# Image parts made one image further ahead, and 13 of 20 instead of 3 of 5 images in the combined form

## The chip, the cores and the metric

The kernel runs on one core of one Trainium2 chip. The metric is the device time of one execution in microseconds. The engines are named as the profile names them: PE is TensorE, PEld its weight loads, DVE is VectorE, ACT is ScalarE, POOL is GpSimd, and SP is the engine whose queue issues most of the DMAs.

## The reference

The input is 160 images of 128 channels and 32 x 32 points. Each image is normalised in groups of four channels (no scale or shift is learned), goes through a 3 x 3 convolution with padding 1, and is added to the image. Image k uses set k mod 5 of five sets of weights. The weights come from U through two steps of rounding:

```python
beta = jnp.max(U); alpha = jnp.min(U)
s1 = (beta - alpha) / 3.0
v1 = s1 * floor(U / s1)
s2 = s1 / 5.0
v2 = s2 * floor((U - v1) / s2)
w = (v1 + v2).reshape(128 * 5, 128, 3, 3)
xb = x.reshape(32, 5 * 128, 32, 32)      # gn(x) here: (g - mean) / sqrt(var + 1e-5), 32 groups
act = conv(xb, w, padding=1, feature_group_count=5)
out = x + act.reshape(160, 128, 32, 32)
```

## The kernel before

**Order of the images.** The kernel takes the images of set 0 first, then those of set 1, and so on: image i of the kernel is image i mod 32 of set i // 32. The loop in `run` has one step for each image, and all instructions are put on the engines' queues in the order in which that loop writes them; the framework adds the waits between engines from the tiles that they share. So what stands behind what on an engine is decided by the order in a step.

**Parts of an image.** The matmuls take 16-bit operands, so a normalised image is split in a high part and a low part (what the high part leaves over). An image takes one of two forms, chosen by `combined(i)`.

- *Not combined.* POOL makes the normalised image `z` (in `beside_pairs`; for the first image of a group of images ACT does it in `normalise`, with `shift` and `rstd`). ACT copies it to the high part `hi` (`high_part`). DVE makes the low part `lo` (`low_part`) and its sums and differences of neighbouring rows, `rows` (`combinations`). PE runs the high part with nine taps in each of two halves, and only the low part through the sums of rows, which need fewer products: 30 matmuls in all.
- *Combined.* The sums and differences are made first, in 32 bits, from the image itself: POOL makes part of `v` (`beside_pairs`, `outer_columns`), DVE the rest (`combine`). ACT makes the high part `vh` of all of it (`high_combined`) and DVE the low part `vl` (`low_combined`). Both parts go through the sums: 24 matmuls.

In both forms `sums_of_pairs` puts six or twelve matmuls into the banks m1a or m1b (by turns) and m2. ACT copies m2 out (`leave`), DVE makes the start of the even and odd halves of the result from both (`pairs`), PE adds the rest (`main`), and ACT copies the result out (`residual`, L926). POOL then issues a DMA that adds it to the output in memory (`accumulate`), to which SP has before stored the input itself (`store_input`).

**A step.** In step i PE makes the sums of pairs of image i+1 and `main` of image i. The parts are made ahead: `beside_pairs` and `combine` for image i+4, the high part for i+3, the low part for i+2. DVE's order in a step is: the low part of i+2, `pairs` of i+1, `combine` of i+4. ACT's order is: the sums of a later image, the result of i-1, m2 of i+1, the high part of i+3, the squares of the later image.

**Statistics.** ACT makes a sum and a sum of squares for each image (`measure`), eight early images go to DVE. `STAT_LEAD` and the expression `10 + i // 4` say how far ahead. Images come in groups (two, two, then fours up to 24, then eights) whose mean and deviation are made together in three later steps by small operations on PE, ACT, POOL and DVE. In late groups DVE ends them with `scales_by_vector` (L307, L309), which also makes `shift`.

**Weights.** The weights of a set are prepared during the set before it, in small DVE and ACT operations that `later.take` puts into the steps one by one at an even pace.

**Buffers and loads.** An image pair is one chunk of 1 MB in one of `CHUNKS` = 12 buffers. `consumed(c)` says from which step on a chunk's buffer is taken for another load. In SP's queue a load waits until the buffer's last readers are done and its store has landed; the store of a chunk waits for its load.

Of the kernel before, what the change touches and what calls it, by code (L numbers as in the profile page):

```python
# [11 lines left out]
ALU = mybir.AluOpType  # L12
# [9 lines left out]
NB = 2  # L22
# [152 lines left out]
def last_of(steps, last=None):  # L175
    for last in steps:
        pass
    return last
# [27 lines left out]
class Statistics:  # L206
# [5 lines left out]
    def __init__(self, nc, small, gavg, mhalf, nb, scale, name):  # L212
        self.nc, self.small, self.gavg, self.mhalf = nc, small, gavg, mhalf
        self.nb, self.scale, self.name = nb, scale, name
        self.late = False

        self.mv = self.tile("mv", [nb, 2])

# [85 lines left out]
    def scales_by_vector(self):  # L304

        vector = self.nc.vector
        vector.tensor_scalar_mul(self.rstd, self.rstd, self.scale)  # L307
        self.shift = self.tile("shift", [self.nb])
        vector.tensor_tensor(self.shift, self.ngm, self.rstd, ALU.mult)  # L309

    def scales(self):
        nc = self.nc
# [72 lines left out]
class Main:  # L385
# [21 lines left out]

    STAT_LEAD = 14  # L410
    LOAD_LEAD = 18
    CHUNKS = 12
    STEADY = 7
    BY_VECTOR = (8, 10, 11, 14, 19, 24, 29, 34)
    FIFTHS = 30
# [10 lines left out]
    def __init__(self, tc, ctx, keep, x, u, out):  # L426
        self.tc = tc
        nc = self.nc = tc.nc
        self.imgs, C, self.H, self.W = x.shape
        P = self.P = nc.NUM_PARTITIONS  # L430
        assert C == P and self.H * self.W == 1024
        self.per_set = self.imgs // N_SETS
        self.xv = x.rearrange("(b n) c h w -> n c b (h w)", n=N_SETS)
        self.ov = out.rearrange("(b n) c h w -> n c b (h w)", n=N_SETS)
        self.uv = u.rearrange("n (o i k) -> n o i k", o=C, k=TAPS)

        def pool(name, bufs, **kw):
            return ctx.enter_context(tc.tile_pool(name=name, bufs=bufs, **kw))

        self.const = pool("const", 1)  # L440
        self.qpool = pool("quant", 1)
        self.wpool = pool("weights", 2)
        self.upool = pool("u", 1)
        self.xpool = pool("x", self.CHUNKS)
        self.zpool = pool("z", 2)
        self.parts = pool("parts", 4)
        self.rows = pool("rows", 4)
        self.wide = pool("wide", 2)
        self.wide_parts = pool("wide_parts", 3)
        self.evac = pool("evac", 2)  # L450
        self.sums = pool("sums", 3)
        self.unread = pool("unread", 1)
        self.small = pool("small", 3)
        self.ps_eo = pool("ps_eo", 2, space=PSUM)
        ps_m = pool("ps_m", 1, space=PSUM)
        ps_small = pool("ps_small", 1, space=PSUM)
        self.steps = Steps(nc, keep)

        self.m1a, self.m1b, self.m2_ps = (
            ps_m.tile([P, self.H // 2, self.W], F32, tag=name, name=name)  # L460
            for name in ("m1a", "m1b", "m2")
        )
        self.pair = [self.m1a, self.m2_ps]

        small = ps_small.tile([P, 512], F32, tag="small", name="small")
        self.pt, self.pg = small[:, : ROW * P].rearrange("p (k o) -> p k o", k=ROW), small[:, ROW * P :]
        self.chunks, self.z, self.hi, self.v, self.eo, self.m2 = {}, {}, {}, {}, {}, {}
        self.sum, self.stored = {}, {}
        self.tables, self.wts, self.across = {}, {}, {}
        self.columns = []  # L470

        cuts = [0, 2, 4, 8, 12, 16, 20, *range(24, self.imgs + 1, 8)]
        self.groups = [range(a, b) for a, b in zip(cuts, cuts[1:])]
        self.group_of = {i: k for k, g in enumerate(self.groups) for i in g}
        self.stats = {}
# [131 lines left out]
    def stats_of(self, k):  # L607
        if k not in self.stats:
            self.stats[k] = Statistics(
                self.nc, self.small, self.gavg, self.mhalf, len(self.groups[k]),  # L610
                self.steps.lift, k,
            )
            self.stats[k].late = self.groups[k].start not in self.HURRIED
        return self.stats[k]

    def measure(self, i, stages=(0, 1)):
# [31 lines left out]
    def combined(self, i):  # L648

        if i < self.STEADY or i >= self.imgs:  # L650
            return False

        if i < self.FIFTHS:
            return i % 2 == 1
        return i % 5 % 2 == 0 if i < self.THIRDS else i % 4 != 2

    def by_scalar_too(self, i):

# [301 lines left out]
    def store_input(self, c):  # L960
# [6 lines left out]
            return  # L967
        self.stored.update((i, self.store(i)) for i in images)

    def consumed(self, c):  # L970

        return max(i + 2 if self.by_hand(i) else i - 2 for i in range(c * NB, c * NB + NB))

    def run(self):
        nc, P = self.nc, self.P
# [130 lines left out]
        for i in range(self.imgs):  # L1106
# [30 lines left out]
            else:  # L1137
                j = i - 1
                self.conv(i, on_the_way)
            ahead = i + min(10 + i // 4, self.STAT_LEAD + 1)  # L1140
            to_measure = range(measured, min(self.imgs, ahead))
            measured += len(to_measure)
            if i == 2:
# [30 lines left out]
            else:  # L1174

                last = None
                if self.combined(i + 2):
                    last = last_of(self.low_combined(i + 2))
                elif i + 2 < self.imgs:
                    self.low_part(i + 2)  # L1180
                    later.take(1)
                    last = last_of(self.combinations(i + 2))
                last = later.take(2 if self.combined(i + 2) else 1, last)
                if i + 4 < self.imgs:
                    before = self.last_but_one(last)
                    for st in scaled:
                        self.after(st.power(), before)
                    self.beside_pairs(i + 4, before)
                if i > self.FIRST and self.by_hand(j):
                    self.residual(j)  # L1190
                for k in by_scalar:
# [1 line left out]
                if i > self.FIRST and not self.by_hand(j):  # L1193
                    self.residual(j)
                    self.accumulate(j)
                part = i + 3 < self.imgs and not self.combined(i + 3)
                if i + 1 < self.imgs:
                    self.leave(i + 1)
                for st in ready:
                    if not st.late:  # L1200
                        st.deviations()
                if part:
                    if self.by_scalar_too(i + 3):
                        self.normalise(i + 3)
                    self.high_part(i + 3)
                if self.combined(i + 3):
                    self.high_combined(i + 3)
                for k in by_scalar:
                    self.measure(k, (1,))
            for st in middle:  # L1210
# [13 lines left out]
            if i >= self.FIRST:  # L1224

                if i + 1 < self.imgs:
                    self.pairs(i + 1)
                for st in scaled:
                    st.scales_by_vector()
                if self.combined(i + 4):  # L1230
                    self.combine(i + 4)
                else:
                    later.take(1)
                later.take_scalar()
                if b in (self.per_set - 4, self.per_set - 2):
                    later.finish()
                for st in ready:
                    if st.late:
                        st.deviations_by_vector()
# [65 lines left out]
```

## Time and profile before

| | us |
|---|---|
| median of 3 runs (968.45 to 969.02) | 968.95 |
| profiled execution, its own time | 968.17 |
| its span, first to last instruction | 966.4 |
| PE busy | 926.9 |
| DVE busy | 910.1 |
| ACT busy | 862.0 |
| POOL busy | 463.6 |

PE's busy time counts the time in which at least one matmul runs; matmuls overlap, and their ends are modelled. The granted clock of TensorE is 0.998 of full speed. The DMA engines are busy nine tenths or more in 32 of the 40 slices of the span, and move 263 GB/s in the mean. A load of 1 MB lands in the median 12.7 us after it is issued, a store of 1 MB 18.6 us. The time of an instruction in a row of the profile is its own duration; the next one of its engine can start up to some 0.1 us before its end.

### The profile page before, as it was taken

Reading aid. Unit: us, or ns where it says so; the run is one execution under the profiler, and the core shown is the slowest. Engines: PE = TensorE matmul, PEld = TensorE weight load, DVE = VectorE, ACT = ScalarE, POOL = GpSimd, SP = SyncE. Lnnn points to the kernel's source line nnn. Section 1 sums busy time; section 2 is a strip of 40 time slices with the busy share of each in tenths; the row PEclk is TensorE's granted clock in tenths of the full one; section 3 lists DMA queues with packets and bytes.
Section 4 is the critical chain, followed back from the end, with each engine's and each line's share of the span. In section 5 each row is a group of like instructions: output and inputs, shape, how many; then the busy total and the mean of one; then the engine's idle time right before and its main releaser. Section 6 shows DMA issues by size and latency. Waiting matters only on the chain.

```text
span 966.4 us, 13055 instructions
## 1 busy us (share of the span) xinstructions
PE 926.9 (96%) x4432; PEld 433.6 (45%) x4432; DVE 910.1 (94%) x1280; ACT 862.0 (89%) x1167; POOL 463.6 (48%) x477
## 2 busy tenths in 40 slices
PE   2999999999999999999999999999999999999997
PEld 1444444444444444444444444444444444444443
DVE  7999999999999999989999999999999998998995
ACT  5879999999999999999989999999989999998561
POOL 4345344446445444554355435534445545666550
PEclk9999999999999999999999999999999999999999
DMA  9079999999999999999999999999999999666663
GB/s 363 20 273 340 338 328 321 334 322 315 327 320 328 314 327 323 311 315 258 283 243 287 276 305 286 278 251 301 278 274 260 286 275 255 98 90 107 91 107 112
DMA packets 67450, 254.22 MB, mean 263 GB/s; under 512 B 5296, under 2 KB 5296, under 8 KB 67376
## 3 DMA queue, kind: packets, MB, share of 16 engines
q1 hardware_dynamic: 45344, 173.09, 47.6%
q0 software_dynamic: 22032, 80.23, 44.7%
q8 instruction: 36, 0.59, 0.2%
q14 instruction: 38, 0.31, 0.1%
HBM read 89.19 MB, written 164.10 MB: 262 GB/s over the span
## 4 chain that ended last, share of the span: by engine, by line


## 5 line engine op out<-in xcount | busy, mean ns | idle before, releaser
L785 PE MATMUL eo<-hi,wt 128*128 128x496 f16 (+3 forms) x1170 | 310.3, 375 | 0.9 <-ACT wt L567 0.9
L840 PEld LDWEIGHTS <-wt 128*128 128x128 f16 x1884 | 183.9, 99 | 211.5 <-DVE rows L770 1.7
L741 DVE SCALAR_TENSOR_TENSOR vl<-v,rstd,vh 128x2048 f16<-128x2048 f32 x94 | 221.5, 2356 | 1.0 <-ACT vh L735 0.9
L840 PE MATMUL eo<-vh,wt 128*128 128x512 f16 x561 | 210.2, 375 | 0.2 <-DVE eo L902 0.2
L840 PE MATMUL eo<-vl,wt 128*128 128x512 f16 x561 | 210.1, 375 | 0.0
L735 ACT ACTIVATE vh<-v,rstd 128x2048 f16<-128x2048 f32 x94 | 188.1, 2001 | 13.4 <-DVE v L694 13.0
L926 ACT COPY sum<-eo 128x1024 f32<-128x1024 f32 x153 | 160.7, 1050 | 29.4 <-PE eo L840 28.5
L675 POOL TENSOR_SCALAR v<-xt,ngm 128x64 f32<-128x64 f32 x94 | 83.0, 883 | 215.5 <-issue 66.8
L785 PEld LDWEIGHTS <-wt 128*128 128x128 f16 x1242 | 120.9, 99 | 140.2 <-DVE eo L902 2.6
L248 ACT ACTIVATE junk<-xt,mv 128x1024 uint8<-128x1024 f32 x152 | 174.4, 1147 | 0.1
L840 PEld LDWEIGHTS <-across 128*128 128x128 f16 x1128 | 110.3, 98 | 140.3 <-issue 13.3
L241 ACT ACTIVATE junk<-xt 128x1024 uint8<-128x1024 f32 x152 | 160.5, 1056 | 13.8 <-DMA xt<-in_x_dram 10.7
L711 POOL TENSOR_SCALAR z<-xt,ngm,rstd 128x1024 f32<-128x1024 f32 x49 | 90.5, 1847 | 155.9 <-DVE rows L769 45.9
L840 PE MATMUL eo<-rows,wt 128*128 128x512 f16 x378 | 143.5, 380 | 0.0
L950 POOL DMA_DIRECT2D out_dram<-sum x153 | 133.8, 876 | 9.5 <-ACT sum L926 6.1
L840 PE MATMUL m<-vl,across 128*128 128x496 f16 (+1 forms) x282 | 105.6, 374 | 9.5 <-DVE vl L741 9.5
L687 DVE TENSOR_TENSOR v<-xt 128x960 f32<-128x960 f32 x94 | 109.0, 1160 | 0.0
L840 PE MATMUL m<-vh,across 128*128 128x496 f16 (+1 forms) x282 | 105.6, 375 | 0.9 <-ACT m L888 0.9
L888 ACT ACTIVATE m<-m 128x512 f32<-128x512 f32 x157 | 93.8, 597 | 13.4 <-PE m L840 13.2
L705 POOL TENSOR_TENSOR v<-xt 128x512 f32<-128x512 f32 x94 | 97.2, 1034 | 0.0
L748 DVE TENSOR_TENSOR lo<-z,hi 128x1024 f16<-128x1024 f32 x66 | 80.6, 1220 | 0.0
L286 POOL TENSOR_TENSOR rstd<-ve,mhalf 128x8 f32<-128x8 f32 (+2 forms) x24 | 39.1, 1629 | 68.8 <-DVE rows L769 22.0
(150 smaller groups left out, 1182.3 us busy)
## 6 DMA issues: line engine op xcount, KB each, us to landing
xt<-in_x_dram SPq DMA_DIRECT2D x78, 1024.0 KB, 12.7
out_dram<-sum POOLq DMA_DIRECT2D x153, 512.0 KB, 8.8
out_dram<-xt SPq DMA_DIRECT2D x76, 1024.0 KB, 18.6
out_dram<-xt SPq DMA_DIRECT2D x7, 512.0 KB, 3.7
u<-in_L_conv_U_dram SPq DMA_DIRECT2D x4, 576.0 KB, 19.0
xt<-in_x_dram SPq DMA_DIRECT2D x4, 512.0 KB, 9.7
range<-in_L_conv_U_dram SPq DMA_DIRECT2D x3, 576.0 KB, 7.9
u<-in_L_conv_U_dram SPq DMA_DIRECT2D x2, 288.0 KB, 3.2
```

What stands on the lines that cost most here:

```text
L241: self.nc.scalar.activation(junk, image, ACTF.Copy, scale=-1.0 / image.shape[1], accum_out=self.mv[:, j, 0:1],)
L248: self.nc.scalar.activation(junk, image, ACTF.Square, bias=self.mv[:, j, 0:1], accum_out=self.mv[:, j, 1:2],)
L687: nc.vector.tensor_tensor(self.view(v, 1, (511, 2), (half, H), (1, half - 1)), self.view(x, 1, (1, 2), (W, H), (2, half - 1)), self.view(x ...
L705: ins = nc.gpsimd.tensor_sub(self.v[i][:, 1536:], odd, even)
L711: ins = nc.gpsimd.tensor_scalar(z, self.image(i), st.ngm[:, j], st.rstd[:, j], ALU.add, ALU.mult)
L735: self.nc.scalar.mul(vh, self.v[i], st.rstd[:, j])
L741: yield self.nc.vector.scalar_tensor_tensor(vl, self.v[i], st.rstd[:, j], self.hi[i], ALU.mult, ALU.subtract)
L785: nc.tensor.matmul(self.bank(target, a)[:, first:end, c0:c1], self.wts[n, col][:, k, :], tile[:, s0 : s0 + 2 * (end - first) - 1 : 2, c0 + ...
L840: self.nc.tensor.matmul(out, weights, moving, start=start and j == 0, stop=False, skip_group_check=True)
L888: self.nc.scalar.mul(m2, self.m2_ps, 0.5)
L926: nc.scalar.copy(self.as_banks(i, self.sum[i]), self.flat(i, eo))
L950: added = self.nc.gpsimd.dma_start(self.ov[n, :, b], self.sum.pop(i), accum_op=ALU.add)
```

## The change

- The parts of an image are made one image further ahead: `step_of(i, ahead)` gives the images for which a step makes a part. For early steps it is image i + ahead. In step 11 (`beside_pairs`, `combine`), 12 (high parts) and 13 (low parts) it is two images, 15 and 16. After these it is i + ahead + 1.
- `combined` takes 13 of 20 images between 30 and 130 instead of 3 of 5: 65 of 100 images instead of 60.
- `shift` is made by `scales_by_vector` only for groups whose first image is not combined; no other image reads it there. Of 19 late groups, 13 begin with a combined image.
- Images are measured one further ahead, and the lead grows faster at the start.
- The pools `rows` and `wide_parts` have one buffer more, the chunks of images one less (11), and a chunk is taken to be consumed one step earlier from image 18 on.
- Later weight steps: one after a low part and one after `combine` where two stood in a row.

```diff
-        self.late = False
+        self.late = self.shifted = False
...
-        self.shift = self.tile("shift", [self.nb])
-        vector.tensor_tensor(self.shift, self.ngm, self.rstd, ALU.mult)
+        if self.shifted:
+            self.shift = self.tile("shift", [self.nb])
+            vector.tensor_tensor(self.shift, self.ngm, self.rstd, ALU.mult)
...
-    STAT_LEAD = 14
+    STAT_LEAD = 15
+    FURTHER = 11
     LOAD_LEAD = 18
-    CHUNKS = 12
+    CHUNKS = 11
...
-        self.rows = pool("rows", 4)
+        self.rows = pool("rows", 5)
...
-        self.wide_parts = pool("wide_parts", 3)
+        self.wide_parts = pool("wide_parts", 4)
...
+            self.stats[k].shifted = not self.combined(self.groups[k].start)
...
-        return i % 5 % 2 == 0 if i < self.THIRDS else i % 4 != 2
+        return i * 13 % 20 < 13 if i < self.THIRDS else i % 4 != 2
...
+    def step_of(self, i, ahead):
+        change = self.FURTHER + 4 - ahead
+        return [k for k in range(i + ahead + (i > change), i + ahead + 1 + (i >= change)) if k < self.imgs]
...
-        return max(i + 2 if self.by_hand(i) else i - 2 for i in range(c * NB, c * NB + NB))
+        return max(i + 2 if self.by_hand(i) else i - 2 - (i > self.FURTHER + 6) for i in range(c * NB, c * NB + NB))
...
-            ahead = i + min(10 + i // 4, self.STAT_LEAD + 1)
+            ahead = i + min(10 + i // 3, self.STAT_LEAD + 1)
...
-                if self.combined(i + 2):
-                    last = last_of(self.low_combined(i + 2))
-                elif i + 2 < self.imgs:
-                    self.low_part(i + 2)
-                    later.take(1)
-                    last = last_of(self.combinations(i + 2))
-                last = later.take(2 if self.combined(i + 2) else 1, last)
-                if i + 4 < self.imgs:
+                for k in self.step_of(i, 2):
+                    if self.combined(k):
+                        last = last_of(self.low_combined(k), last)
+                    else:
+                        self.low_part(k)
+                        later.take(1)
+                        last = last_of(self.combinations(k), last)
+                last = later.take(1, last)
+                if last:
                     before = self.last_but_one(last)
                     for st in scaled:
                         self.after(st.power(), before)
-                    self.beside_pairs(i + 4, before)
+                    for k in self.step_of(i, 4):
+                        self.beside_pairs(k, before)
...
-                if part:
-                    if self.by_scalar_too(i + 3):
-                        self.normalise(i + 3)
-                    self.high_part(i + 3)
-                if self.combined(i + 3):
-                    self.high_combined(i + 3)
+                for k in self.step_of(i, 3):
+                    if self.combined(k):
+                        self.high_combined(k)
+                        continue
+                    if self.by_scalar_too(k):
+                        self.normalise(k)
+                    self.high_part(k)
...
-                if self.combined(i + 4):
-                    self.combine(i + 4)
-                else:
+                for k in self.step_of(i, 4):
+                    if self.combined(k):
+                        self.combine(k)
                     later.take(1)
```

More of the change, by code (lines that the diff above doesn't have):

```diff
@@ L1195, in run @@
                     self.accumulate(j)
-                part = i + 3 < self.imgs and not self.combined(i + 3)
                 if i + 1 < self.imgs:
```

## The prediction

> **What bounds the kernel now.** I read the page's busy line first, then the spacing of the matmuls in the timeline, then the busy time of three stretches, then the waits inside the long one. The page's first part (busy us, share of the span, instructions):
>
> ```profile
> PE 926.9 (96%) x4432; PEld 433.6 (45%) x4432; DVE 910.1 (94%) x1280; ACT 862.0 (89%) x1167; POOL 463.6 (48%) x477
> ```
>
> Three engines stand near full, so a share of the whole span decides nothing. I cut the span at the starts of `pairs` of images 3, 30, 131 and 158: the middle stretch is the one in which images 30 to 130 are made. The busy time of each engine in them:
>
> ```profile
> 56.40:222.40 166.00, 162.19 (x781) 75.85 (x780) 162.69 (x257) 153.12 (x214) 75.50 (x82) 1.00 1.04 335
> 222.40:791.80 569.40, 564.66 (x2708) 264.04 (x2707) 548.37 (x752) 545.55 (x744) 272.74 (x267) 1.00 1.02 293
> 791.80:951.70 159.90, 157.00 (x749) 73.21 (x747) 146.51 (x171) 127.38 (x153) 90.41 (x78) 1.00 0.69 126
> ```
>
> The columns are length, PE, PEld, DVE, ACT, POOL, granted clock, DMA share, GB/s. In the middle PE is idle 4.7 of 569.4 us, DVE 21.0, ACT 23.9. In the last stretch PE is idle 2.9 of 159.9 and DVE 13.4. In the first DVE is idle 3.3 of 166 and PE 3.8. So PE sets the pace from image 30 on, with DVE 3% behind it; before that DVE and PE share it. Who waits in the middle stretch (us in total, times, longest):
>
> ```profile
> DVE eo L900 <- ACT m L888: 6.0, 6, 1.4
> ...
> PE m L840 <- DVE vl L741: 4.7, 4, 1.9
> ...
> DVE twice L296 <- ACT wt L567: 3.2, 4, 1.3
> DVE eo L900 <- PE m1b L840: 2.7, 4, 1.2
> ```
>
> PE's whole idle time is one kind: the first products of an image wait for its low part `vl`, which DVE makes in the step just before. The same wait is 2.9 us (3 times) in the last stretch and 1.9 us in the first. DVE's waits are on PE, or on ACT's copy of what PE made. The small gaps between DVE's instructions are the rest: 21.0 less some 14.3 in gaps over 0.15 us leaves 6.7.
>
> **What the Trainium skill says.** "TensorE: Matmul & The Clock Gate", section "Wait — 56ns, not 53.3ns?", puts back-to-back warm matmuls at N/2.4 GHz plus about 2.5 ns, 216 ns for 512 columns. The trace agrees: twelve matmuls of a combined image start from 380.07 to 382.60, 0.211 us apart (496 and 512 columns). PE is really full, not only busy by a modelled end. "SBUF — State Buffer", section "SBUF: two separate sides", says that a DVE operation with two SBUF inputs and a GpSimd operation exclude each other for a whole instruction. The trace agrees, in the lines on `shift` below. "Perfetto Trace Analysis", section "Tensor Engine Instruction (MATMUL, LD_WEIGHTS)", says that ACT and DVE are strict first-in first-out: a late operand stops all behind it, which no run here contradicts.
>
> **The change part by part.**
>
> *Five more combined images (65 for 60 between 30 and 130).* A combined image needs 24 matmuls (two sources, `vh` and `vl`; 12 for the sums of pairs, 12 in `main`), another 30 (6, and 18 + 6). So 30 matmuls go; at the trace's 0.212 us that is **6.4 us less on PE**. DVE pays. The rows of the middle stretch:
>
> ```profile
> L741 DVE SCALAR_TENSOR_TENSOR vl<-v,rstd,vh 128x2048 f16<-128x2048 f32 x60 | 141.9, 2364 | 0.6 <-ACT vh L735 0.5
> L687 DVE TENSOR_TENSOR v<-xt 128x960 f32<-128x960 f32 x60 | 69.0, 1150 | 0.0
> L748 DVE TENSOR_TENSOR lo<-z,hi 128x1024 f16<-128x1024 f32 x40 | 48.7, 1217 | 0.0
> L694 DVE SCALAR_TENSOR_TENSOR v<-xt,twice 128x512 f32<-128x512 f32 x60 | 44.7, 744 | 0.0
> ```
>
> Combined: 2.36 + 1.15 + 0.74 = 4.26 us. Not combined: 1.22 + 0.69 (L761) + 2 x 0.42 (L769, L770) = 2.74. Five times 1.52 is **7.6 us more on DVE**. ACT: 2.00 (L735) for 1.04 (L645), five times, is +4.8; the group starts 48, 56, 88, 96 and 128 were not combined and become so, 32 and 72 and 112 the other way, so two of the 1.24 us `normalise` (L637) go: +2.3 net, inside its 23.9 idle. POOL: five times 0.90 + 1.03 for `v`, and three fewer `z` of 1.85 at most: +4 us, inside 297 of idle time.
>
> *`shift` no longer made for 13 of 19 late groups, ten of them in the middle.* Its row L309 there has 12 at a mean of 498 ns. But the timeline shows what these are:
>
> ```profile
> 443.76 1.03 POOL L705 TENSOR_TENSOR v<-xt 128x512 f32<-128x512 f32 x1
> ...
> 443.86 0.96 DVE L309 TENSOR_TENSOR shift<-ngm,rstd 128x8 f32<-128x8 f32 x1
> ...
> 444.75 1.15 DVE L687 TENSOR_TENSOR v<-xt 128x960 f32<-128x960 f32 x1
> ```
>
> `shift`, eight columns wide, ends as POOL's L705 ends; where POOL is quiet it takes 0.17 and the next starts 0.09 after it. The next, L687, has two SBUF inputs as well and would stand in the same place. So a `shift` is worth 0.09 (the block moves) to 0.50 us (it is gone), ten of them 1 to 5. I take **1 us**, since nothing in the edit moves POOL.
>
> *Parts one image further ahead from 15 or 16 on.* Step 11 does `beside_pairs` and `combine` for 15 and 16, step 12 ACT's high parts of both, step 13 the low parts of both; afterwards everything is as far apart as before, except that PE takes a part one step later (5.7 us). This takes away PE's waits for `vl`: at most 4.7 + 2.9, and in the first stretch 1.4 of the 1.9 (the other 0.5 is image 15's, whose low part stays in step 13). `rows` and `wide_parts` get one buffer more, as a part lives one step longer; that costs nothing in time. Cost: one image's low part (2.4 to 2.7 us) is pulled into a stretch where DVE has 1.2 us of gaps over 0.15, and comes back only at the end, where PE is the bound and gains nothing. If all of DVE's gaps take it, +1; if it pushes PE fully, +4 with the `combine` made early (1.9, half of the time). I take **+2**. The steeper lead of the sums and squares (`i // 3`) brings at most two images' ACT work (2 x 2.2 us) forward into ACT's 12.9 idle there: 0, at worst +4.
>
> *11 chunks for 12, each freed one image earlier.* SP's order puts load 18 behind two more 1 MB stores than before, and the image is measured one step earlier. Before, load 18 was issued at 120.3, load 19 at 135.2 and load 20 at 150.0, with 28 to 33 us to landing; moved two stores on, loads 18 and 19 stand where 19 and 20 stood, land near 163 and 178, and are wanted near 168 and 181. So a margin of 3 to 5 us where there were some 20; from load 24 on the order of the queue is the old one and 10 us remain. I take 0. If a load is late, ACT stops in its measurement with the copies and high parts of that step queued behind it, and PE waits for those: 2 to 5 us in all.
>
> *`later.take`* is spread: one weight step after the low part and one after `combine`, for two in a row. No instruction more, 0; a gain of under 1 us, from waits of a step on the one before it, is possible.
>
> **The sum**, against the profiled execution's 968.17 (966.4 span and 1.8 around it). Middle: PE's floor is 564.7 - 6.4 = 558.3. DVE's is 548.4 + 6.7 (small gaps) + 7.6 - 1 = 561.7: DVE takes over as the bound. Its waits for `wt` (3.2) have nothing to do with the change and stay: 564.9, against 569.4, is -4.5. First stretch +2. Last stretch -2.5 of its 2.9. Together -5, so 963.2; the median of 968.95 is 0.8 above the profiled execution, so **964**.
>
> **Rivals.**
> - *PE stays the bound.* The further lead lets DVE ride out its heavy steps, the `shift` savings are whole (5 us), and DVE runs with few waits: middle 558.3 to 561, last -2.9, first 0: 954 to 959. For it: all of PE's idle time had one cause, which goes. Against: DVE at 98 to 99% must meet PE twice in each step (`pairs`).
> - *DVE's waits do not shrink (the slower one).* `pairs` of an image needs PE's sums and ACT's copy m2, wherever the parts stand. If DVE's gaps over 0.15 us in the middle stay at 14.3 us, the middle takes 561.7 + 14.3 = 576.0, +6.6, and with +2 and -2.5 the kernel 975. It decides from 9 us of such gaps on: 561.7 + 9 + 2 - 2.5 is the old time. For it: 8.7 of the 14.3 are at L900, which the lead doesn't touch. Against: DVE waits there because it is early, and it will be late.
> - *Loads late* in steps 19 to 25: the forecast plus 2 to 5, 966 to 969.
> - *That it does nothing* is out: 30 matmuls are gone from PE's order.
>
> **How the numbers follow.** Forecast 0.50 (960 to 967), PE the bound 0.22, DVE's waits stay 0.18, loads late or a dearer beginning 0.10. A measurement of this kernel tells about 0.2% (1.9 us) from no change. Faster by more: all of the second, 0.46 of the first, 0.04 of the last: 0.72. Within: 0.04 of the first, 0.04 of the third, 0.05 of the last: 0.13. Slower: 0.14 of the third and 0.01 of the last: 0.15. The range 956 to 972 leaves out the best of the second and the worst of the third; the forecast's own is 960 to 967.
>
> **What would show it.** In the profile after: 30 matmuls fewer; PE's waits for `vl` gone from image 16 on; the middle some 4 to 5 us shorter with DVE's idle time down from 21 to about 10 and PE's waits for `eo` of L902 up; L687 taking some 2 us where `shift` stood; no ACT wait for `xt` after step 15. I am wrong if DVE's gaps stay above 9 us, if PE idles under 3 us in the middle, or if the first stretch grows by more than 4.

## The result, and the profile after

| us | before | after |
|---|---|---|
| median | 968.95 | 966.80 |
| lowest to highest | 968.34 to 969.48 | 965.63 to 968.85 |
| profiled execution | 968.17 | 968.85 |
| its first, middle and last stretch, and what follows the last | 166.0, 569.4, 159.9, 14.7 | 171.7, 566.8, 156.8, 15.4 |

The ratio of the times is 0.998, 95% interval 0.9972 to 0.9989: 2.15 us faster, where 5 were forecast. The profiled execution of after is the slowest of its nine. The stretches sum up (the first cut lies at 56.4 us in both): +5.7 - 2.6 - 3.1 + 0.7 = +0.7, which is 968.85 - 968.17. (The prediction calls its cuts the starts of `pairs` of images 3, 30, 131 and 158; its times are those of images 3, 30, 130 and 159, and the same images cut the stretches here.)

The page of after, busy time of each engine:

```profile
PE 922.9 (95%) x4402; PEld 430.0 (44%) x4402; DVE 913.2 (94%) x1262; ACT 863.6 (89%) x1165; POOL 469.3 (49%) x484
```

The 30 matmuls are gone (4432 to 4402). The three stretches of after (length, PE, PEld, DVE, ACT, POOL, granted clock, DMA share, GB/s):

```profile
56.40:228.10 171.70, 164.71 (x778) 75.84 (x777) 166.25 (x260) 157.89 (x220) 71.96 (x83) 0.98 1.04 338
228.10:794.90 566.80, 559.37 (x2683) 261.15 (x2682) 553.49 (x736) 547.00 (x742) 286.01 (x276) 1.00 1.02 287
794.90:951.70 156.80, 156.80 (x748) 73.13 (x747) 140.81 (x166) 122.71 (x148) 87.26 (x76) 1.00 0.71 141
```

In the middle PE works 5.3 us less than before and idles 7.4 instead of 4.7; DVE works 5.1 more and idles 13.3 instead of 21.0. In the last stretch PE never stops. The waits of the middle stretch (total, times, longest):

```profile
PEld L843 <- DVE eo L905: 12.0, 10, 2.1
...
PE eo L843 <- DVE eo L905: 7.3, 9, 1.6
DVE eo L903 <- ACT m L891: 4.4, 4, 1.3
```

No wait of PE for `vl` is left there. All of PE's idle time is now a wait for the second half of `pairs` (L905; L902 before), as the prediction said a DVE-bound middle would look. DVE's waits of 3.2 us for `wt`, which the prediction kept, are gone too.

The two rows of DVE that grew, middle stretch of after (busy, mean ns, idle before):

```profile
L744 DVE SCALAR_TENSOR_TENSOR vl<-v,rstd,vh 128x2048 f16<-128x2048 f32 x65 | 152.4, 2344 | 0.0
L690 DVE TENSOR_TENSOR v<-xt 128x960 f32<-128x960 f32 x65 | 81.6, 1256 | 0.1
```

L690's mean went from 1150 to 1256 ns, because in eight of 65 cases, at 1.92 to 2.00 us, it stands where `shift` stood. One of them in the timeline of after (start, duration):

```profile
308.61 1.03 POOL L708 TENSOR_TENSOR v<-xt 128x512 f32<-128x512 f32 x1
308.68 1.99 DVE L690 TENSOR_TENSOR v<-xt 128x960 f32<-128x960 f32 x1
```

POOL's operation ends at 309.64, and L690 needs its usual 1.15 us from about there: the block moved, as forecast.

**The beginning.** It grew by 5.7 us, not 2. That isn't an accident of this slowest execution: in e4 and e5 below, whose kernels begin alike, `pairs` of image 30 stands 5.2 and 4.9 us later than before. Two places carry it. Step 6 measures two images instead of one (`i // 3`): DVE then stands 2.36 us on ACT's copy of m2, and `pairs` of image 8 starts at 92.4 instead of 89.5. Steps 12 and 13 hold more of DVE's work than before; DVE and PE there:

```profile
125.86 1.15 DVE L690 TENSOR_TENSOR v<-xt 128x960 f32<-128x960 f32 x1
126.93 0.74 DVE L697 SCALAR_TENSOR_TENSOR v<-xt,twice 128x512 f32<-128x512 f32 x1
...
129.81 2.34 DVE L744 SCALAR_TENSOR_TENSOR vl<-v,rstd,vh 128x2048 f16<-128x2048 f32 x1
132.07 1.22 DVE L751 TENSOR_TENSOR lo<-z,hi 128x1024 f16<-128x1024 f32 x1
132.20 0.38 PE L843 MATMUL m<-vl,across 128*128 128x512 f16 x1 [2.43 <-DVE vl L744]
...
136.95 1.44 PE L788 MATMUL eo<-hi,wt 128*128 128x512 f16 x3 [1.10 <-DVE eo L905]
```

The long stop, 2.43 us, waits for `vl` of image 15, which stood in step 13 before the change too; PE waited 0.54 us for it then. What is new ahead of it on DVE is `combine` of image 17 (L690 and L697, 1.7 us), pulled forward into step 12, and 0.5 us of a group's deviations (L296 to L302), also one step earlier. The second low part of step 13, that of image 16, comes behind (L751 at 132.07): it delays `pairs` of image 14, for which PE waits the 1.10 us.

And right behind the long stop TensorE's granted clock halves (stretches of after, clock third from the end):

```profile
124.50:132.00 7.50, 4.60 (x22) 1.82 (x20) 7.36 (x16) 7.50 (x10) 2.18 (x3) 1.00 1.04 328
132.00:134.00 2.00, 1.80 (x8) 0.74 (x8) 2.00 (x4) 2.00 (x6) 0.00 (x0) 0.84 1.04 274
134.00:136.00 2.00, 1.85 (x5) 0.44 (x3) 2.00 (x5) 0.92 (x2) 0.73 (x1) 0.50 1.03 422
136.00:138.00 2.00, 1.05 (x3) 0.44 (x4) 1.97 (x3) 1.35 (x2) 1.44 (x2) 0.50 1.03 422
138.00:140.00 2.00, 2.00 (x6) 0.74 (x5) 2.00 (x3) 1.97 (x4) 0.70 (x1) 0.50 1.02 420
140.00:142.00 2.00, 2.00 (x11) 0.85 (x10) 1.93 (x5) 0.02 (x1) 1.99 (x4) 0.95 1.06 369
```

For some 6.8 us the matmuls start 0.41 to 0.43 us apart instead of 0.21: at most 3.4 us of PE's time. `pairs` of image 16 starts at 146.8 instead of 138.0; image 30 is only 5.7 late, so part of it is made up later.

### The profile page after: what moved, and what is told of

Same layout as the page of the kernel before. It is cut to its first block, busy times and chain, and to the rows that moved or that the text cites. A ratio compares the mean times of both kernels' runs of the same rounds, so it can differ in the third digit from the quotient of the medians.

```text
span 967.1 us, 12979 instructions
## 1 busy us (share of the span) xinstructions
PE 922.9 (95%) x4402; PEld 430.0 (44%) x4402; DVE 913.2 (94%) x1262; ACT 863.6 (89%) x1165; POOL 469.3 (49%) x484
## 4 chain that ended last, share of the span: by engine, by line
## 5 line engine op out<-in xcount | busy, mean ns | idle before, releaser
L788 PE MATMUL eo<-hi,wt 128*128 128x496 f16 (+3 forms) x1080 | 287.6, 377 | 1.8 <-DVE eo L905 1.1
L843 PEld LDWEIGHTS <-wt 128*128 128x128 f16 x1884 | 183.2, 99 | 220.5 <-DVE eo L905 13.5
L744 DVE SCALAR_TENSOR_TENSOR vl<-v,rstd,vh 128x2048 f16<-128x2048 f32 x99 | 232.0, 2343 | 0.2 <-ACT vh L738 0.2
L843 PE MATMUL eo<-vh,wt 128*128 128x496 f16 (+1 forms) x591 | 221.5, 375 | 7.9 <-DVE eo L905 7.9
L843 PE MATMUL eo<-vl,wt 128*128 128x496 f16 (+1 forms) x591 | 221.3, 375 | 0.0
L738 ACT ACTIVATE vh<-v,rstd 128x2048 f16<-128x2048 f32 x99 | 198.2, 2002 | 10.4 <-DVE v L697 10.1
L843 PEld LDWEIGHTS <-across 128*128 128x128 f16 x1188 | 116.5, 98 | 140.4 <-issue 6.3
L788 PEld LDWEIGHTS <-wt 128*128 128x128 f16 x1152 | 112.5, 100 | 131.5 <-DVE eo L905 3.7
L843 PE MATMUL eo<-rows,wt 128*128 128x512 f16 x348 | 132.5, 381 | 0.0
L690 DVE TENSOR_TENSOR v<-xt 128x960 f32<-128x960 f32 x99 | 123.2, 1244 | 0.1
L751 DVE TENSOR_TENSOR lo<-z,hi 128x1024 f16<-128x1024 f32 x61 | 74.5, 1221 | 0.0
```

The lines of the kernel that those rows point to most:

```text
L690: nc.vector.tensor_tensor(self.view(v, 1, (511, 2), (half, H), (1, half - 1)), self.view(x, 1, (1, 2), (W, H), (2, half - 1)), self.view(x ...
L738: self.nc.scalar.mul(vh, self.v[i], st.rstd[:, j])
L744: yield self.nc.vector.scalar_tensor_tensor(vl, self.v[i], st.rstd[:, j], self.hi[i], ALU.mult, ALU.subtract)
L788: nc.tensor.matmul(self.bank(target, a)[:, first:end, c0:c1], self.wts[n, col][:, k, :], tile[:, s0 : s0 + 2 * (end - first) - 1 : 2, c0 + ...
L843: self.nc.tensor.matmul(out, weights, moving, start=start and j == 0, stop=False, skip_group_check=True)
```

## The experiments

Edits are against the kernel named. Times are medians over several executions; ratios are to the kernel before, run beside it (968.7 to 968.9 us), with 95% intervals. Two runs whose intervals overlap aren't told apart by their medians alone. "Stretches" are first, middle and last of the profiled execution (before: 166.0, 569.4, 159.9; after: 171.7, 566.8, 156.8).

### One part of the change undone

**e1_ramp**, on after: the old growth of the measuring lead up to step 8.

```diff
-            ahead = i + min(10 + i // 3, self.STAT_LEAD + 1)
+            ahead = i + min(10 + i // (4 if i < 9 else 3), self.STAT_LEAD + 1)
```

> The changed kernel, but with the old lead of the measurements (i // 4) up to step 8, so that step 6 measures one image and not two. Theory (the beginning costs 5.6 us more, and 2.9 of it is this double measurement, behind which ACT's copy of m2 came 2.4 us late): 964.0, the start of pairs of image 8 back near 89.5, and no wait of DVE on ACT there. Rival (the beginning is dearer because of late loads or the double low part alone; ACT's delay would only have moved a wait): 966.3 to 967.3.

965.16 us, 0.9962 (0.9948 to 0.9975); 167.4, 567.1, 156.8. By the medians the early ramp costs the changed kernel 1.6 us (the intervals just touch), about half of what was expected here, against the 0 of the prediction. In the trace the mechanism is as expected: `pairs` of image 8 starts at 88.6, and DVE has no wait there.

**e2_late_start**, on after: the double step at images 28 to 30 (`FURTHER = 28` for 11).

> The changed kernel, but the step forward by one image is made in steps 28 to 30 (images 32 and 33 together), where VectorE was idle 29% of a step in the kernel before, and not in steps 11 to 13. Theory (the double low part of step 13 stops TensorE for 4 us because VectorE has nothing to spare there, and TensorE's clock then drops): 963.5 to 965, granted clock 0.998, no wait of TensorE above 1.4 us in the first stretch. Rival (VectorE's work must be paid wherever it stands): 966 to 967.5, the stop only moves to step 30.

967.34, 0.9984 (0.9978 to 0.9991); 166.1, 568.0, 156.8. By the median the rival came true: nothing is gained, as when the pulled-in work has to be paid wherever it stands. The profiled execution (964.49) is one of the fastest of 21 and doesn't show where the median is lost. In it image 30 is 1.2 us later than before, and PE's idle time in the middle is 10.0 instead of 7.4, part of it one stop behind `pairs` (2.1 us) right after the double step. The step in which DVE idled 29% before was that between `pairs` of images 33 and 34; in steps 28 to 30 it idled under 5%.

The steep ramp is in this kernel and in e3 too, and up to step 10 their loops write what after's writes. Yet `pairs` of image 8 waits for ACT's copy 0.17 us here and 1.34 in e3, against 2.36 in after. ACT had stood 0.53, 1.71 and 1.93 us on a load of U just before, and in after 0.92 us more on POOL. So what the ramp costs depends on how late ACT already is.

**e3_no_lead**, on after: no further lead at all (`FURTHER = 1000`).

> The changed kernel with the parts never made further ahead (13 of 20 combined, shift left out, 11 chunks and the lead of the measurements stay). Theory (the lead takes away TensorE's waits for vl, 4.7 and 2.9 us, and costs 3.5 at the beginning; without it the heavier VectorE makes the waits longer): 970 to 972, with the waits for vl back in the middle at 6 us or more. Rival (the waits for the second half of pairs are what vl's were, only renamed, and the lead is worth nothing): 965 to 967.

968.48, 0.9999 (0.999 to 1.0007). Its middle and last stretch, and PE's wait in the middle:

```profile
223.20:795.00 571.80, 560.68 (x2683) 261.54 (x2682) 553.94 (x740) 549.53 (x742) 285.26 (x275) 1.00 1.01 288
795.00:951.50 156.50, 156.50 (x747) 73.02 (x746) 143.05 (x168) 124.15 (x149) 88.98 (x78) 1.00 0.74 142
```

```profile
PE m L843 <- DVE vl L744: 10.4, 12, 2.0
```

In the middle the waits for `vl` are back and longer than before the change, so there the lead does what it was said to do; with 13 of 20 it gains 1.7 us in all by the medians, less than the theory expected. But the last stretch has none, without any lead. What the prediction gave to the further lead there came from another part.

**e4_three_fifths**, on after: 3 of 5 combined again.

```diff
-        return i * 13 % 20 < 13 if i < self.THIRDS else i % 4 != 2
+        return i % 5 % 2 == 0 if i < self.THIRDS else i % 4 != 2
```

> The changed kernel with the old choice of combined images, 3 of 5. Theory (TensorE still sets the pace in the middle: it gets 6.4 us more of work and loses some 4 of its 7.4 us of idle time): 969 to 970. Rival (VectorE has become the bound of the middle, and 7.6 us less for it are worth as much as 6.4 more for TensorE): 966 to 967.5, TensorE idle under 1 us in the middle.

966.14, 0.997 (0.9962 to 0.9979). Its middle stretch:

```profile
227.60:794.00 566.40, 565.18 (x2713) 264.60 (x2712) 543.94 (x746) 546.78 (x745) 277.08 (x268) 1.00 1.02 288
```

PE has 5.8 us more to do and idles 1.2 instead of 7.4: the same length. The rival came true: the five more combined images are worth nothing that can be measured.

**e5_shift_kept**, on after: `shift` always made (`shifted = True`).

> The changed kernel, but shift is made in all late groups as before. Theory (a shift costs more than the 0.09 us of the prediction: in the kernel without the further lead the last stretch is 3.4 us shorter too, and its three waits for vl stood 3 to 4 us behind the three shifts there): 968.5 to 970, middle and last stretch together 3 us or more longer, though with the lead the wait in the last stretch may be on pairs. Rival (the block by POOL moves to the next operation, the prediction): 966.8 to 967.6.

967.91, 0.9987 (0.998 to 0.9994); 170.0, 567.9, 156.9. Leaving out 13 `shift`s is worth 1.1 us by the medians, 0.085 each, though the intervals overlap; e6 (0.8 us for 11 of them) and e16 (1.3 us) agree. That is near the 0.09 us forecast for an operation whose block moves to the next one.

### Parts alone, and two doubts about the beginning

**e6_before_no_shift**, on before: `shift` left out where nothing reads it, as in the diff, nothing else.

> The kernel before, with only shift left out where nothing reads it (3 of 5 combined there: 11 of 19 late groups). Theory (shift alone takes away the three waits for vl of the last stretch): 965 to 966.3, the last stretch 2.9 us shorter, no wait of TensorE in it. Rival (it is the order of the weight steps or the lead of the measurements that did it in the last stretch): 968.2 to 968.7, and the three waits of 0.97 us stay.

968.09, 0.999 (0.9983 to 0.9997); 166.1, 568.9, 159.7. The last stretch keeps its three waits for `vl` (2.7 us): L689, which is L687 of before, takes 1.99 us where `shift` stood. So it isn't the missing `shift` that shortened it; that theory fell.

**e7_before_13of20**, on before: 13 of 20 alone.

```diff
-        return i % 5 % 2 == 0 if i < self.THIRDS else i % 4 != 2
+        return i * 13 % 20 < 13 if i < self.THIRDS else i % 4 != 2
```

> The kernel before, with only 13 of 20 images combined. Theory (without the lead VectorE's heavier steps come late for TensorE, so the 6 us taken off TensorE are given back as waits for vl): 970 to 972, middle 571 to 573, waits for vl in it 9 us or more. Rival (the part is worth what TensorE loses, as the prediction had it in the main): 964 to 965.

977.5, 1.0086 (1.007 to 1.0102). Its middle stretch, and PE's wait in it:

```profile
221.60:801.00 579.40, 563.54 (x2684) 261.41 (x2683) 558.10 (x749) 550.25 (x743) 285.15 (x275) 1.00 1.01 289
```

```profile
PE m L840 <- DVE vl L741: 15.0, 14, 2.6
```

Alone it costs 8.7 us, more than the theory expected.

**e8_ramp_35_split**, on after: e1 and e4, and the second low part of step 13 put behind `pairs`.

```diff
-                for k in self.step_of(i, 2):
+                lows = self.step_of(i, 2)
+                for k in lows[:1]:
...
                     self.pairs(i + 1)
+                for k in lows[1:]:
+                    if self.combined(k):
+                        run(self.low_combined(k))
+                    else:
+                        self.low_part(k)
+                        run(self.combinations(k))
```

> Three edits on the changed kernel: measurements by i // 4 up to step 8, 3 of 5 combined, and in step 13 the second low part put behind pairs. Theory (the stop of TensorE in step 13 is the start of pairs coming late behind two low parts; behind pairs, the second has a step of slack): 961.5 to 963, no half clock near 130 to 150 us, first stretch under 167. Rival (the 2.7 us of low part must be paid by a later pairs): 964 to 965, the stop and the half clock stand a step later.

965.02, 0.9953 (0.994 to 0.9967); 168.9, 566.3, 157.0. The theory fell. PE's stop for `vl` of image 15 is 1.79 us, as in e1, and the clock still halves for 3.4 us behind it; only the wait for `pairs` of image 14 (0.94 us in e1) is gone. So the long stop comes from what stands ahead of image 15's low part, not from the second low part.

**e9_before_takes**, on before: weight steps spread as in the change.

```diff
-                last = later.take(2 if self.combined(i + 2) else 1, last)
+                last = later.take(1, last)
...
-                else:
-                    later.take(1)
+                later.take(1)
```

> The kernel before, with only the weight steps spread as in the changed kernel (one after the low part, one after combine, for two in a row). Theory (13 of 20 alone made the kernel 8.7 us slower, and with this spread, without the further lead, only level: two weight steps behind a combined low part make the next low part late): 966 to 967.5, the middle 566.5 to 568, waits for vl in it under 3 us. Rival (the spread only matters with 13 of 20): 968.3 to 969, waits for vl 4 us or more.

968.47, 0.9996 (0.9988 to 1.0005); 165.8, 570.6, 160.0, waits for `vl` in the middle 4.6 us. Nothing gained; the rival came true. (The profiled execution is the slowest of 13: its clock is halved for 3.4 us at 498.)

**e10_old_takes**, on after: the old places of the weight steps (the reverse of e9).

> The changed kernel with the old places of the weight steps (two in a row behind a combined low part, none behind combine). Theory (the spread carries the change, not the further lead alone): 970 to 974, TensorE's waits on pairs in the middle 12 us or more. Rival (with the lead a low part has a step of slack and the places of the weight steps do not count): 966.3 to 967.5.

969.1, 1.0006 (0.9997 to 1.0014); 171.3, 570.3, 156.8. Here the spread is worth 2.3 us by the medians, less than the theory said, more than the rival. PE waits 8.4 us for `pairs` in the middle, not 12 or more, against 7.3 in after. That two weight steps in a row delay `pairs` fits, but the profiled execution, the slowest of 13, can't show it: its clock is halved three times for 3.4 us (at 92, 137 and 369), each time behind a stop of PE.

**e11_before_lead15**, on before: one constant.

```diff
-    STAT_LEAD = 14
+    STAT_LEAD = 15
```

> The kernel before, with only the lead of the measurements 15 for 14. Theory (the last stretch is 3 us shorter without lead and with shift kept, so it comes from the step in which a group's scales are made: one step earlier it no longer meets the low part of a not combined image): 965.5 to 966.5, last stretch 156.5 to 157, no wait for vl in it. Rival (the buffers or the places of the weight steps did it): 968.5 to 969, three waits of 0.97.

**964.35**, 0.9954 (0.994 to 0.9967): faster than the whole change. Its stretches:

```profile
56.40:224.20 167.80, 162.80 (x784) 76.07 (x782) 162.77 (x257) 155.74 (x218) 75.38 (x82) 1.00 1.04 336
224.20:790.80 566.60, 564.13 (x2707) 263.96 (x2706) 551.21 (x751) 545.32 (x744) 271.36 (x267) 1.00 1.02 293
790.80:947.50 156.70, 156.70 (x749) 73.12 (x748) 143.61 (x171) 125.05 (x149) 88.86 (x78) 1.00 0.72 129
```

PE does as much work as before in the middle and idles 2.5 us instead of 4.7; in the last stretch it idles 0 instead of 2.9. So this one constant gives all of the last stretch's gain and as much in the middle as after has.

**e12_before_takes_lead15**, on before: e9 and e11.

> The kernel before with both: weight steps spread and the lead of the measurements 15. No part is made further ahead, 3 of 5 combined, 12 chunks, shift kept. Theory (these two small edits hold most of what the change gains, without its dear beginning): 963 to 965, below the changed kernel. Rival (the further lead is what gains): 966.5 or more.

964.35, 0.9953 (0.9939 to 0.9966); 168.3, 566.7, 156.8. As e11: with 3 of 5 and no further lead the spread is worth nothing. Which of the two makes it count in e10 isn't separated.

### Why the measuring lead does it

A lead of one image more moves the late groups' scales (L307, L309) one step earlier: from the steps of `pairs` 133, 141, 149 to 132, 140, 148. What stands behind them on DVE, in the timeline of before:

```profile
811.17 0.37 DVE L307 TENSOR_SCALAR rstd<-rstd,lift 128x8 f32<-128x8 f32 x1 [0.22 <-POOL rstd L286]
811.58 0.96 DVE L309 TENSOR_TENSOR shift<-ngm,rstd 128x8 f32<-128x8 f32 x1
812.46 1.15 DVE L687 TENSOR_TENSOR v<-xt 128x960 f32<-128x960 f32 x1
813.53 0.74 DVE L694 SCALAR_TENSOR_TENSOR v<-xt,twice 128x512 f32<-128x512 f32 x1
814.20 2.34 DVE L741 SCALAR_TENSOR_TENSOR vl<-v,rstd,vh 128x2048 f16<-128x2048 f32 x1
...
816.59 0.38 PE L840 MATMUL m<-vl,across 128*128 128x512 f16 x1 [0.97 <-DVE vl L741]
```

and in that of e11:

```profile
804.47 0.22 DVE L307 TENSOR_SCALAR rstd<-rstd,lift 128x8 f32<-128x8 f32 x1
804.73 0.17 DVE L309 TENSOR_TENSOR shift<-ngm,rstd 128x8 f32<-128x8 f32 x1
804.82 1.15 DVE L687 TENSOR_TENSOR v<-xt 128x960 f32<-128x960 f32 x1
805.89 0.74 DVE L694 SCALAR_TENSOR_TENSOR v<-xt,twice 128x512 f32<-128x512 f32 x1
806.55 1.22 DVE L748 TENSOR_TENSOR lo<-z,hi 128x1024 f16<-128x1024 f32 x1
```

Before, the scales take 1.3 us ahead of the `vl` of a combined image, and PE waits 0.97 for it. In e11 the next low part is that of an image that isn't combined, 1.22 us instead of 2.34, and the scales take 0.35. (The expectation of e11 has this the wrong way round, and so has that of e14: it is lead 14 that meets a combined low part. The last stretch of e11 came out as expected all the same, its whole time lower.) From image 130 on one image of four (remainder 2) isn't combined and groups come by eights, so the scales meet the same place in the pattern every time. The next runs ask whether it is this phase or the lead as such.

In the middle stretch of before the trace shows the same picture. PE's two longest stops there, 1.94 us each, stand behind the scales of `pairs` 77 and 117, again with `combine` and a combined `vl` between; one of them:

```profile
496.83 0.38 PE L840 MATMUL m<-vl,across 128*128 128x512 f16 x1 [1.94 <-DVE vl L741]
```

They are 3.9 of PE's 4.7 us of idle time. In e11, where these scales come behind `pairs` 76 and 116, no wait for `vl` in the middle is longer than 0.9 us. No run tests this stretch from the other side.

**e13_before_lead16** and **e14_before_lead18**, on before: `STAT_LEAD = 16` and 18.

> The kernel before with the lead of the measurements 16. Theory (what counts is the step of the scales: two steps earlier than before they meet, in the last stretch, a combined low part and no combine, the lightest of the four): last stretch 156.5 to 157.2 without a wait for vl, as with 15, and the middle not longer than before's 569.4: 963.5 to 966. Rival (it is margin, and more margin gains more): below 963.5. Third (15 was a stroke of luck in the middle alone): 967 or more.

> The kernel before with the lead of the measurements 18. Theory (the step counts): in the last stretch the scales meet a not combined low part and a combine again, as with 14, so 159.5 to 160.2 and three or four waits for vl of 0.9 to 1.0 us. Rival (margin): last stretch 156.5 to 157.2 and no wait. The whole: 966 to 970 by the theory, 963 to 965 by the rival.

16: 964.15, 0.9952 (0.9939 to 0.9966); 167.6, 567.2, 156.0, no wait for `vl` in the last stretch. 18: 971.46, 1.003 (1.0019 to 1.004); 167.9, 573.1, 157.2, with two waits for `vl` there (1.9 us). 18 puts the scales at `pairs` 129, 137, ..., four before those of lead 14 and so at the same place in the pattern. That more lead brings the waits back speaks for the phase. The theory expected three or four waits and 159.5 to 160.2 in the last stretch; there are two because the scales at 129 fall ahead of its cut. The whole, 971.46, is longer than the theory said.

**e15_lead15_13of20**, on before: e11 and e7.

> The kernel before with lead 15 and 13 of 20 combined, nothing else. Theory (VectorE is as full as TensorE, and without the further lead the 6 us taken off TensorE come back as waits for vl): 968 to 974, waits for vl in the middle 9 us or more. Rival (the loss of 13 of 20 alone came from the scales' step too): 961 to 964.

971.56, 1.003 (1.0019 to 1.004); 167.5, 573.6, 156.7, with 10.3 us of waits for `vl` in the middle (12 times). With lead 15 as well, 13 of 20 costs 7.2 us where parts aren't made further ahead.

**e16_lead15_no_shift**, on before: e11 and e6.

> The kernel before with lead 15 and shift left out where nothing reads it. Theory (shift is worth 0.5 to 1 us, as between the changed kernel with and without it and on the kernel before): 963.3 to 963.9. Rival (nothing is left for it once the waits are gone): 964.2 to 964.7.

**963.05**, 0.994 (0.9926 to 0.9953); 167.5, 566.1, 156.5. The best of all kernels here: 5.7 us below before and 3.75 below after. The missing `shift` is worth 1.3 us by the medians of five executions each.

**e17_before_lead17**, on before: `STAT_LEAD = 17`.

> The kernel before with STAT_LEAD 17, which puts the last scales of the statistics in the steps of pairs 130, 138, 146, 154 (remainder 2 of 4). There DVE has a combine and a low part of a combined image behind them, and another such pair of heavy operations just ahead. Theory (what counts is whether the scales fall on a step with heavy DVE work, which comes back with a period of four images): the waits of PE for vl are back in the last stretch, 2 to 3 us in all, as with lead 14 and 18. Rival (a longer lead is what removes them, and 18 was too long for another reason): no such wait in the last stretch, as with 15 and 16.

967.92, 0.9988 (0.9982 to 0.9995); 167.9, 570.4, 156.0, no wait for `vl` in the last stretch. The theory as stated missed. Behind `pairs` 130 stand low parts of two combined images (132 and 133) and then a light one; behind 133, those of three (135, 136, 137); behind 131 and 132, one and none. Waits came with three, not with two or fewer. This sharper form was found after the run, and no later run tests it.

**e18_before_other_fourth**, on before, lead 14: of the images 130 to 155 those that aren't combined are 131, 135 and so on to 155, instead of 130, 134 and so on to 154.

```diff
-        return i % 5 % 2 == 0 if i < self.THIRDS else i % 4 != 2
+        return i % 5 % 2 == 0 if i < self.THIRDS else i % 4 != (3 if i < 156 else 2)
```

> The kernel before with STAT_LEAD 14 as it was; from image 131 to 155 the image that is not combined is the one with remainder 3 of 4 instead of 2; as many combined images as before. Theory: the scales stay in the steps of pairs 133, 141, 149, but the low part behind them is now that of an image that is not combined (1.2 us instead of 2.3), so PE's waits for vl behind them (2.9 us in the last stretch) are gone and the last stretch takes 156.5 to 157.5 instead of 159.9: 965.5 to 966.5. Rival (the lead as such, not the phase): nothing changes there, 968 to 969.

965.82, 0.9971 (0.9958 to 0.9983); 166.2 and 569.8 in the first and middle stretch, as before. Its last stretch:

```profile
792.40:948.60 156.20, 156.20 (x746) 72.91 (x744) 143.60 (x170) 126.61 (x153) 88.44 (x78) 1.00 0.69 132
```

Lead 14, as many combined images, the scales where they were: PE's waits there are gone (behind the scales at 810.52 the next low part of DVE is L748, at 812.65) and the kernel is 3.0 us faster. So the last stretch is a matter of phase, and this is shown from both sides: by moving the scales and by moving the pattern.

## Why the prediction was wrong, point by point

By the medians, the kernel's way from before to after is: 968.8; lead 15 alone 964.35 (-4.4); `shift` left out 963.05 (-1.3); further lead, steeper ramp, 11 chunks and spread weight steps, still 3 of 5 (e4), 966.14 (+3.1, of which the ramp is about 1.6); 13 of 20 966.8 (+0.7, not clear of noise). The direction was right, by luck: most of the gain came from a constant that the prediction put at nothing, `shift` gave the 1 us forecast, and the rest together lost. The steps that failed are the waits left in the middle (3.2 us forecast, 8.6 measured), the cost of the beginning (+2 us forecast, +5.7 measured) and the lead of the measurements, put at nothing (-4.4).

- **The middle: -4.5, measured -2.6. The waits that are left were mis-sized.** The sum was 555.0 us of DVE's work, 6.7 of small gaps and 3.2 of waits for `wt`: 564.9. Measured were 553.5, 4.7 and 8.6. DVE's waits at `pairs` (8.7 before) were taken as gone once DVE is the bound; 6.4 stayed, while those for `wt` went. The rival of DVE's waits had this in view. (It decides from 8.2 us of such gaps on, not 9: 561.7 + 8.2 + 2 - 2.5 is the old 569.4.)
- **The five more combined images.** The amounts were nearly right (PE -5.3 for -6.4, DVE +5.1 for +6.6). By the prediction's own floors they gain nothing once PE's waits for `vl` are gone: 564.7 on PE without them, 564.9 on DVE with them. They did gain nothing (e4), but in another way: with 3 of 5 PE idles 1.2 us, with 13 of 20 PE idles 7.4 and DVE 13.3. What was taken from PE came back as waits: for `vl` without the further lead (e7 +8.7, e15 +7.2), for `pairs` with it.
- **"This takes away PE's waits for `vl`" in the middle: credited to the wrong part.** At 3 of 5 the measuring lead alone takes 2.7 us off the middle (e11); with it in place and `shift` left out the middle is 566.1 us without the further lead (e16) and 566.4 with it and the rest of the bundle (e4). The further lead only repairs part of what 13 of 20 costs (e3 against after, 1.7 us).
- **The same in the last stretch: -2.5. Right in size (-3.1), wrong in cause.** The lead was given it by argument. e3 has no lead and no wait there; e11 and e18 show the phase of the scales.
- **STAT_LEAD 14 to 15 was left out of the sum.** It was read as a part of the ramp. A value that says when periodic work happens is a change of its own: -4.4 here, +2.7 at 18.
- **The beginning: +2, bound +4. It measured +5.7** in the profiled execution, the largest miss of the sum there, and the third of the prediction's signs of being wrong (a first stretch longer by more than 4). The ramp at 0 failed: 1.6 us (e1). PE's wait for `vl` of image 15 was to stay at 0.5 us; it became 2.43, since the `combine` made early stands ahead of it. The pulled-in work was priced as displaced work of DVE only, not as stops of PE with a halved clock behind them. Image 30 is 1.8 us late with lead 15 alone (e11) and 0.8 with lead 15 and the steep ramp (e3), so these parts don't add up singly.
- **Spread weight steps: 0, "a gain of under 1 us".** 2.3 us in the changed kernel (e10), nothing in the one before (e9).
- **Right:** `shift` (1 us forecast, 1.1 measured, its block moved to L690); no late loads with 11 chunks (ACT has no wait for `xt` behind step 4); ACT's and POOL's added work hidden; `vl` waits replaced by waits for `pairs`.

Open: why the middle stretch takes 566.7, 567.2, 570.4 and 573.1 us at leads 15 to 18. There the pattern repeats by fives against groups of eight, so no lead hits one place always; it wasn't taken apart. (The cut moves too: the last stretch holds 749, 745, 743 and 738 matmuls.) Nor is the width of after's times explained (3.2 us over nine, 1.1 for before). The halved clock alone doesn't do it: the execution of 968.59 us had a mean granted clock of 0.996, that of 966.57 one of 0.994.

## What to carry to other kernels

Where two engines that feed each other are both near full, as PE and DVE here, don't price a shift of work between them by the larger floor: look which handover waits, and count the work moved as no gain unless the receiving engine's idle time is shown to be usable. Small periodic work costs little by itself and much by where it falls; before restructuring, try its phase with one constant. And undo each part of a bundle alone: here one line of it was worth twice the whole.

## What the hardware showed unexpectedly

Behind a short stop of PE inside a full kernel its clock can halve. In the 7.5 us up to 132.0 in after PE was busy 4.6 us, and its longest single gap was 2.43; the clock fell at 133.3. The Trainium skill ("TensorE: Matmul & The Clock Gate", section "What's actually happening") lets the clock fall after an idle window of some 3.4 us; no gap here is that long, so by the measurement less is enough. The duration at half clock was 3.4 us in nine cases and 6.8 in after, one and two times the length of that window; that this is more than a coincidence isn't shown.

It doesn't belong to the further lead: in e7 and e9, which are built on before, the clock also fell to half for 3.4 us, behind single stops of 2.20 and 2.09 us.

Between 56 and 952 us all profiled executions together show ten such falls, each during a stop of 1.79 to 2.43 us or within 1.2 us of its end, and none elsewhere. But twelve stops of 1.79 us or more have no halved clock behind them, one of them of 2.56 us (e7). So the length of the stop alone doesn't decide it, and what does stays open. At half clock 3.4 us hold back at most 1.7 us of matmuls, 6.8 us at most 3.4.
